# Attention's side jobs in a four-layer Flamingo kernel: stages written by an estimate of each engine's progress instead of by counts of ticks

## The chip, the cores and the metric

The kernel runs on one core of one Trainium2 chip. The metric is device time in microseconds (us), of which lower is better. The kernel is one program with one launch; it reads all its inputs from the chip's memory and writes its output there.

## The reference, cut to what matters

Sixteen batches of 128 tokens with 256 features go through four layers. Each layer adds a gated attention to a second sequence (`ctx_1024`) and then a gated feed-forward part. All arithmetic is in float32.

```python
x = x + tanh(g_xattn[0]) * L0_xattn(ctx, layernorm(x), ctx)   # 16 heads, width 16
x = x + tanh(g_ffn[0])   * L0_ffn(layernorm(x))               # 8 experts, top 2, hidden 1024, gelu
x = x + tanh(g_xattn[1]) * L1_xattn(layernorm(x), ctx, ctx)   # softmax over the queries
x = x + tanh(g_ffn[1])   * L1_ffn(layernorm(x))               # a dense product and 8 gated LoRA experts
x = x + tanh(g_xattn[2]) * L2_xattn(ctx, ctx, layernorm(x), mask)
x = x + tanh(g_ffn[2])   * L2_ffn(layernorm(x))               # 8 experts, top 2, swiglu, and a shared expert
x = x + tanh(g_xattn[3]) * L3_xattn(ctx, layernorm(x))        # 8 heads of 64; keys from ctx and from x
x = x + tanh(g_ffn[3])   * L3_ffn(layernorm(x))               # 8 experts, top 2, silu

# one of the expert parts: a router, the two best experts of a token, their outputs weighted
gate = softmax(x @ w_gate.T); scores, idx = top_k(gate, 2)
cw = (one_hot(idx, 8) * scores[..., None]).sum(1)
h = gelu(einsum('td,edh->teh', x, W1) + b1)
out = einsum('ted,te->td', einsum('teh,ehd->ted', h, W2) + b2, cw)
```

## The kernel before, in words

**Batches, blocks and steps.** The sixteen batches lie in four blocks of four (`NBLK`, `BPB`). One function, `attend` (L1302), writes the attention of a layer, and it is called three times: for layer 0, for layers 1 and 2 one after the other ("the middle"), and for layer 3. It goes through steps. Step n writes the scores of batch n (`scores`: products L1211 into `ps_s`, exponentials L1221 and L1226 into `e`), the values of batch n-1 (`values`: products L1266 of `e` with `v`, then with `ones` for the row sums, a reciprocal L1277, and `oT`, L1274 or L1279), and the output of batch n-2 (`output`: product L1287 into `ps_y`, then additions into the residual `x`, L362 and L366, and the layer norm's statistics in `ready`). On POOL the row sums are kept in `sum_range` (L1080). Layer 3 has a class of its own for these, `Fast3`.

**The order is written out by hand.** Inside `attend` TensorE (PE), ScalarE (ACT) and VectorE (DVE) are under `tc.manual_schedule`: they execute their instructions in the order in which Python writes them. GpSimd (POOL) and SyncE (SP) also take theirs in program order, outside the three queues. An instruction that waits holds up all that is behind it on its engine.

**Side jobs.** Between the parts of a step stand the stages of other work, each job a Python generator whose `yield` ends a stage:

- queries and keys of the next block (L1155 to L1181, products L929 and L932, `v` in L941 and L947); in layer 3 `turned`, `projected` and their context (L1820 to L1890);
- the layer norm of a finished block, `ln_block` (L316: `xn` on ACT L306, transposes `ps_ln` L329, copy L333);
- the front of the experts for a finished block, `Moe.front` (L436): the layer norm, router (L413), softmax, two maxima (`hot`, `both` L464), ranks (`ps_rank`, L469), offsets and the list of places `xi` (L505 to L521), eight indirect scatters of the tokens into `xg` in memory (L524, POOL), and after some blocks a plan;
- the LoRA part of layer 1 (`Lora.run`, L1453) and the shared expert of layer 2 (`shared2`, L1521);
- slots of expert work (`slots`, L703). A slot is 128 gathered tokens of one expert: it loads `xr` from `xg` (L752) and the first weights (L1373, 1 MB in layer 0) by SP's queue, transposes `xr` (L785), makes the hidden layer (L1420, L1597 or L1645), then the second product (`ps_e`, L822), and scatters the result (L834). There are 39 slots per expert layer. Layer 0 runs 9 of them early, inside its attention, once the plan of blocks 0 and 1 is there; layer 3 runs 9 and then 8 early; the others come after the attention.

**What sets their order before the change.** `attend` calls `tick()` some six times in each step: between the two halves of the scores and after them, between values and row sums and after them, and in `output`. Each job holds a counter; a tick takes one off, and at zero the next stage is written and its `yield` sets the counter anew (`yield 4`: four ticks on). The argument `most` caps the counter: (5, 1) in layer 0, (99, 1) in the middle, (2, 1) in layer 3, the second number once the last scores are written. `Firm` numbers escape the cap, and `quick` cuts a front's numbers to 3. All jobs run at each tick, as many as there are. A stage is thus written a fixed number of ticks after the one before, whether or not its inputs are there yet by then; and the products of a job stand between the halves of a batch's scores, or between its values and row sums, where their tiles have another shape: scores use 32-row tiles (`32*128`), values 32-column tiles (`128*32`), all else is `128*128`.

Of the kernel before, what the change touches and what calls it, by code (L numbers as in the profile page):

```python
# [19 lines left out]
P = 128  # L20
# [70 lines left out]
def kernel(ctx: ExitStack, tc: tile.TileContext, a: dict, out: bass.AP):  # L91
# [112 lines left out]
    class Firm(int):  # L204
        pass

    def quick(job):

        for n in job:
            yield min(n, 3)  # L210
# [41 lines left out]
    seen = {}  # L252

# [44 lines left out]

    def normalized(srcs, mv, rstd):
# [3 lines left out]
        yield 1  # L303
        xns = stat.tile([P, len(srcs), ROW], F32, tag="xn", name="xn", bufs=3)
        for i, src in enumerate(srcs):
            nc.scalar.activation(  # L306
                xns[:, i, 0:D], src, AF.Identity, bias=nmr[:, i:i + 1], scale=rstd[:, i:i + 1]
            )
            if i == 1:
                yield 1  # L310
# [5 lines left out]
    def ln_block(blk, see=None, own_set=False):  # L316
# [6 lines left out]
        yield Firm(3) if own_set else 4  # L323
        xt = xtpool.tile([P, KC, TB], F32, tag="xnT", name="xnT")
        for pair in range(BPB // 2):
# [8 lines left out]
            yield 1 if pair == 0 else 3  # L334
# [87 lines left out]
    class Moe:  # L422
# [4 lines left out]
        def __init__(self, layer, wg, turn, see=None):  # L427
            self.layer, self.wg, self.turn, self.see = layer, wg, turn, see
            self.carry = region
            self.done = None  # L430
            self.scatters, self.returns, self.weighted = [], [], []
# [4 lines left out]
        def front(self, blk, plan=None):  # L436
# [3 lines left out]
            xns, xnT = yield from ln_block(blk, self.see, own_set)  # L440
# [24 lines left out]
            yield Firm(2) if own_set else 6  # L465
# [37 lines left out]
            yield 3  # L503
            off = small("off")
# [17 lines left out]
            for i in range(BPB):  # L522
                for j in range(2):
# [3 lines left out]
                    ).ins, self.scatters, "scatter")  # L527
            if plan is not None:
                yield 1
                yield from plan()  # L530
            return xnT
# [158 lines left out]
        def slots(self, n, plans, lanes, get, fetch1, fetch2, hidden, nf, far, depth):  # L690
# [149 lines left out]
            while not planned(far):  # L840
                yield 1
# [7 lines left out]
            yield 1  # L849
# [3 lines left out]
            for s in range(n):  # L853
                while not planned(s + far + 1):
                    yield 1
# [11 lines left out]
                yield 1  # L867
# [230 lines left out]
    class Fast16:  # L1098
# [44 lines left out]
        def keys(self, blk):  # L1143
# [3 lines left out]
            for c in range(KC):  # L1147
# [8 lines left out]
                yield 1  # L1156

        def queries(self, blk, before):
# [8 lines left out]
            for c in range(KC):  # L1167
# [13 lines left out]
                yield 2  # L1181

        def scores(self, b, tick):
# [24 lines left out]
            for c in range(KC):  # L1208
# [6 lines left out]
                if c == 0:  # L1215
                    tick()
# [29 lines left out]
            tick()  # L1246
# [7 lines left out]
        def values(self, b, tick):  # L1254
            pool, v = self.pool, self.vs[b % 3]
            es = self.es.pop(b)
            oT = pool.tile([P, KC, S], F32, tag="oT", name="oT")
# [3 lines left out]
            for i in range(1 if self.layer == 1 else 2):  # L1261
# [9 lines left out]
                if i == 0:  # L1271
                    tick()
# [10 lines left out]
        def output(self, b, tick):  # L1283
            oT = self.os.pop(b)
            py = ps_x.tile([P, D], F32, tag="x", name="ps_y")
# [16 lines left out]
    def attend(parts, most=(99, 1), filler=None, open_end=False):  # L1302
# [7 lines left out]
        jobs = []  # L1310
        late = False
        filling = []

        def tick():
            for job in list(jobs) + filling:
                job[1] -= 1
                if job[1] <= 0:
                    try:
                        n = next(job[0])
                        job[1] = n if isinstance(n, Firm) else min(n, most[late])  # L1320
                    except StopIteration:
                        (jobs if job in jobs else filling).remove(job)

        def ahead(att, before, blk):
            made = att.prepare(blk, before(blk) if before is not None else None)
            made = [[job, 0] for job in made]
# [5 lines left out]
                  for blk in range(NBLK)]  # L1332
        with tc.manual_schedule(engines=IN_ORDER):
            ln_exp()
            prepared = ahead(*blocks[0][:2], 0)
            for n in range(len(steps) + 2):
                if n == len(steps) - 1 and open_end:
                    next(filler)
                if n == len(steps):
                    late = True  # L1340
                    if filler is not None:
                        filling.append([filler, 0])
                if n < len(steps):
                    if n % BPB == 0:

                        while any(job in jobs for job in prepared):
                            tick()
                        if n // BPB + 1 < len(blocks):
                            att, before, _, blk = blocks[n // BPB + 1]
                            prepared = ahead(att, before, blk)  # L1350
                    att, b = steps[n]
                    att.scores(b, tick)
                if 1 <= n <= len(steps):
                    att, b = steps[n - 1]
                    att.values(b, tick)
                if n >= 2:
                    att, b = steps[n - 2]
                    att.output(b, tick)
                    if b % BPB == BPB - 1:
                        _, _, behind, blk = blocks[(n - 2) // BPB]  # L1360
                        jobs.append([behind(blk), 0])
            while jobs or (filling and not open_end):
                tick()
# [37 lines left out]
    def slots0(moe, n, plans, lanes, get):  # L1401
# [10 lines left out]
        def hidden(get, w, xT, when):  # L1412
            hT = get("hT", [P, nf, S])
            for half in range(2):
# [13 lines left out]
                yield 1  # L1428
# [5 lines left out]
    class Lora:  # L1434
# [10 lines left out]
        def run(self, blk):  # L1445
# [20 lines left out]
            yield 8  # L1466
# [8 lines left out]
            yield 5  # L1475
            for i, b in enumerate(block(blk)):
# [10 lines left out]
                yield 1  # L1487
# [949 lines left out]
```

## Time and profile before

| what | value |
|---|---|
| median of three runs | 1697.64 us (1696.58 to 1700.13) |
| the profiled execution, its own time | 1650.85 us |
| its span, first to last instruction | 1648.8 us |
| mean clock granted to TensorE | 0.973 of full |
| PE busy | 1536.8 us, 93% of the span |
| DVE busy | 874.5 us, 53% |
| ACT busy | 635.8 us, 39% |
| POOL busy | 319.0 us, 19% |

The profile and the trace record one execution. It is 46.8 us shorter than the median of the timed runs, so differences found in the trace are made against 1650.85 us and then carried over to the median. A row of the profile's groups gives the line and engine of an instruction, the tile that it writes and those that it reads, how often it runs, its busy time, the mean time of one, and the idle time just before it with the engine and line that ended it. The rows of stages that the prediction shows give, for each stretch of time, the busy time of the five engines, the granted clock and the share of the DMA engines.

### The profile page before, as it was taken

The numbers are of one execution on the slowest core, as the hardware profiler recorded it, in microseconds if no ns is written. First come the engines' busy times: TensorE is split into PE (matmuls) and PEld (weight loads), VectorE is DVE, ScalarE is ACT, GpSimd is POOL, SyncE is SP. The second block draws the span as 40 slices with busy tenths as digits, with TensorE's granted clock in tenths as the row PEclk, the third lists the DMA queues.
The fourth block names the chain that finished last, engine by engine and source line by source line (L and its number), as shares of the span: only waits on it lengthen the run. The fifth ranks groups of instructions, "written<-read, shape, count | busy, mean of one in ns | idle before, by whom it ended". The sixth has DMA issues, their size and how long they took to land.

```text
span 1648.8 us, 34904 instructions
## 1 busy us (share of the span) xinstructions
PE 1536.8 (93%) x12803; PEld 1194.4 (72%) x12803; DVE 874.5 (53%) x2860; ACT 635.8 (39%) x1517; POOL 319.0 (19%) x402
## 2 busy tenths in 40 slices
PE   6988999999988999999999999999989999998992
PEld 4677889999455666655459999999946655667892
DVE  3686322422367756764445555556734526466655
ACT  4545433345455455553224333334443333223110
POOL 4132411111600000221100110111150002023431
PEclk8998999999999999999999999999989999998997
DMA  9606584443600000110055413401260000033866
GB/s 337 235 31 199 187 268 155 146 146 93 119 1 1 1 14 14 40 40 26 26 208 163 137 58 106 151 27 34 97 122 1 15 1 27 1 98 123 272 188 207
DMA packets 108200, 169.68 MB, mean 103 GB/s; under 512 B 17129, under 2 KB 78382, under 8 KB 108016
## 3 DMA queue, kind: packets, MB, share of 16 engines
q1 hardware_dynamic: 84176, 112.38, 21.6%
q0 software_dynamic: 20304, 49.66, 9.6%
q10 hardware_dynamic: 3536, 5.25, 0.9%
q8 instruction: 108, 1.77, 0.5%
q14 instruction: 76, 0.62, 0.1%
HBM read 268.81 MB, written 48.18 MB: 192 GB/s over the span
## 4 chain that ended last, share of the span: by engine, by line


## 5 line engine op out<-in xcount | busy, mean ns | idle before, releaser
L1597 PEld LDWEIGHTS ps_w<-xT,w 128*128 128x128 f32 x2304 | 264.0, 192 | 2.5
L1597 PE MATMUL ps_w<-xT,w 128*128 128x128 f32 x2304 | 264.9, 275 | 0.0
L834 POOL DMA_INDIRECT yd<-y,to x117 | 119.2, 1019 | 562.8 <-DVE c L797 285.7
L822 PE MATMUL ps_e<-w,hT 128*128 128x256 f32 x848 | 197.5, 380 | 1.8 <-DVE hT L1502 1.3
L822 PEld LDWEIGHTS ps_e<-w,hT 128*128 128x128 f32 x848 | 154.5, 190 | 21.0 <-DVE hT L1502 2.3
L1605 ACT ACTIVATE u<-ps_w,b 128x128 f32<-128x128 f32 x312 | 89.2, 368 | 172.7 <-PE ps_w L1597 165.4
L1608 DVE SCALAR_TENSOR_TENSOR m<-ps_w,b,u 128x128 f32<-128x128 f32 x312 | 87.7, 344 | 111.0 <-PE ps_w L1597 94.0
L1420 PE MATMUL ps_h<-xT,w 128*128 128x128 f32 x1120 | 134.8, 279 | 7.9 <-DMA w<-in_l_w_dram 6.5
L1420 PEld LDWEIGHTS ps_h<-xT,w 128*128 128x128 f32 x1120 | 132.9, 196 | 11.0 <-issue 4.3
L1425 ACT ACTIVATE hT<-ps_h,b 128x128 f32<-128x128 f32 x312 | 88.9, 373 | 114.3 <-issue 83.5
L524 POOL DMA_INDIRECT xg<-xn,xi x96 | 94.2, 981 | 152.9 <-ACT u L1538 55.0
L1532 PE MATMUL ps_w<-xnT,sw 128*128 128x512 f32 x256 | 111.9, 593 | 0.0
L830 DVE SCALAR_TENSOR_TENSOR y<-ps_e,c,bias 128x256 f32<-128x256 f32 x78 | 37.6, 482 | 126.4 <-PE ps_e L822 125.2
L1080 POOL TENSOR_TENSOR sum_range<-sum_range,rs 128x256 f32<-128x256 f32 x48 | 35.1, 732 | 342.2 <-DVE rs L1277 155.3
L1532 PEld LDWEIGHTS ps_w<-xnT,sw 128*128 128x128 f32 x256 | 47.9, 190 | 57.3 <-issue 50.9
L306 ACT ACTIVATE xn<-x,nmr,rstd 128x256 f32<-128x256 f32 x128 | 67.8, 598 | 30.9 <-DVE nmr L302 30.9
L787 DVE COPY xT<-ps_xr 128x256 f32<-128x256 f32 x117 | 48.5, 417 | 57.7 <-PE ps_xr L785 57.6
L1277 DVE RECIPROCAL rs<-ps_o 128x256 f32<-128x256 f32 x32 | 56.2, 1756 | 42.8 <-PE ps_o L1266 42.8
L1211 PE MATMUL ps_s<-qM,kT 32*128 32x256 f32 x768 | 68.9, 418 | 5.2 <-ACT e L1226 5.2
L1226 ACT ACTIVATE e<-ps_s 128x512 f32<-128x512 f32 x128 | 65.7, 602 | 11.4 <-PE ps_s L1211 11.4
L814 ACT ACTIVATE bias<-b,c 128x256 f32<-128x256 f32 x78 | 40.4, 517 | 73.0 <-DMA b<-in_l_b_dram 28.9
L1854 PE MATMUL ps_qk<-kvx,w_att 128*128 128x512 f32 x128 | 62.7, 624 | 0.6 <-DVE kvx L1841 0.6
(275 smaller groups left out, 2547.6 us busy)
## 6 DMA issues: line engine op xcount, KB each, us to landing
w<-in_l_w_dram SPq DMA_DIRECT2D x156, 1024.0 KB
w<-in_l_w_dram SPq DMA_DIRECT2D x39, 512.0 KB
kT<-in_l_wgu_dram SPq DMA_DIRECT2D x39, 512.0 KB
xg<-zeros POOLq DMA_DIRECT2D x15, 1170.0 KB, 24.0
xr<-xg SPq DMA_DIRECT2D x78, 130.0 KB
b<-in_l_b_dram SPq DMA_DIRECT2D x78, 128.0 KB
kT<-in_l_w_dram SPq DMA_DIRECT2D x39, 256.0 KB
x<-yd POOLq DMA_DIRECT2D x48, 128.0 KB, 4.8
```

Source lines behind the costliest of these rows:

```text
L306: nc.scalar.activation(xns[:, i, 0:D], src, AF.Identity, bias=nmr[:, i:i + 1], scale=rstd[:, i:i + 1])
L524: self.unordered(nc.gpsimd.indirect_dma_start(out=xg[:, :], in_=xns[:, i, :], in_offset=None, out_offset=bass.IndirectOffsetOnAxis(ap=xi[: ...
L822: nc.tensor.matmul(po, lhsT=hT[:, f, :], rhs=lane(s)["w2"][:, f, :], start=(f == 0), stop=(f == nf - 1),)
L834: self.unordered(nc.gpsimd.indirect_dma_start(out=yd[:, :], in_=y, in_offset=None, out_offset=bass.IndirectOffsetOnAxis(ap=to[:, 0:1], axi ...
L1211: nc.tensor.matmul(pss[j][:, 2 * c:2 * c + 2, :], lhsT=self.kT[blk][part, c, tok], rhs=self.qM[blk][part, c, :, tok], start=True, stop=True,)
L1226: nc.scalar.activation(e, pss[j], AF.Exp)
L1420: nc.tensor.matmul(ps[:, i, :], lhsT=w["w1"][:, k, f * P:(f + 1) * P], rhs=xT[:, k, :], start=(k == 0), stop=(k == KC - 1),)
L1425: nc.scalar.activation(hT[:, f, :], ps[:, i, :], AF.Gelu, bias=w["b1"][:, f:f + 1])
L1532: nc.tensor.matmul(ps, lhsT=wt[:, k, f * P:(f + 1) * P], rhs=xnT[:, k, :], start=(k == 0), stop=(k == KC - 1),)
L1597: nc.tensor.matmul(ps[:, f, :], lhsT=wt[:, k, s, f * P:(f + 1) * P], rhs=xT[:, k, :], start=(k == 0), stop=(k == KC - 1),)
L1605: nc.scalar.activation(u[:, f, :], pair[0][:, f, :], AF.Identity, bias=w["b1"][:, i:i + 1])
L1608: nc.vector.scalar_tensor_tensor(m1[:, f, :], pair[1][:, f, :], w["b3"][:, i:i + 1], u[:, f, :], ALU.add, ALU.mult,)
```

## The change

Counters go; an estimate of time comes. While `attend` runs, a callback hands each written instruction to a new class `Clock`, which holds a time for each of the four compute engines and for each tile (when it will be written, until when it is read), and adds a formula's duration per instruction. A stage of a job is now marked by its `yield`: `yield Pe(0)` or `yield Pe(1)` says that the stage that follows writes products to PE, a plain number that it doesn't. `Pe(1)` waits in the estimate for what the last stage made, `Pe(0)` doesn't. The rules:

- a stage without products is written at any tick (`poll`) as soon as the estimated PE time has passed the estimated end of its inputs;
- a stage with products is written only at whole ticks (`whole`): one ahead of a step's scores, one after its output; and only until a budget of `share` us of PE time per step is used up: 2.5 in layer 0, 5.0 in the middle, 8.0 in layer 3;
- the ticks inside the scores, between scores and values, and between values and row sums become `tick(False)`, which only polls;
- ahead of the values (`until(v, *es)`) and of the output (`until(oT)`) ready PE stages are written as long as the estimate says that those tiles aren't there yet (`idle`), the filler too;
- `urgent` writes, ahead of the values, ready PE stages of a finished block's job, where `hurry` is set (it is, in all three calls);
- at most two jobs of finished blocks are open at once (`waiting`), the third begins when the first has ended; a front takes up the running offsets only when the front before it has finished (`self.passed`), `xn`'s three buffers are handed on only when released (`held`), and layer 2's block is held until layer 1's LoRA part of that block has been written (`through`);
- early slots of layer 0 wait by `while not started: yield Pe(1)`.

What is computed, the tiles, the loads and the number of instructions of each kind stay as they were; their order changes. The core of the diff:

```diff
-    def attend(parts, most=(99, 1), filler=None, open_end=False):
...
-        def tick():
-            for job in list(jobs) + filling:
-                job[1] -= 1
-                if job[1] <= 0:
-                    try:
-                        n = next(job[0])
-                        job[1] = n if isinstance(n, Firm) else min(n, most[late])
+    class Clock:
...
+        def note(self, ins):
+            outs, srcs = self.aps(ins.outs), self.aps(ins.ins)
...
+            if "DMA" in type(ins).__name__ or ins.engine not in self.at:
+                end = max(start, self.at[PE]) + 3.0
+                self.moved.append(end)
+            else:
+                start = max(start, self.at[ins.engine])
+                end = start + self.cost(ins, outs[0], srcs)
+                self.at[ins.engine] = end
+                end += 0.2 if ins.engine == PE else 0.1
+                self.ends.append(end)
...
+    def attend(parts, filler=None, open_end=False, hurry=True, share=2.5):
...
+        def run_stage(job):
+            clock.ends, clock.moved = [], []
+            try:
+                n = next(job[0])
...
+            job[2] = isinstance(n, Pe)
+            ends = clock.ends or clock.moved
+            if not ends:
+                job[1] = now() + (0.5 if n else 0.0)
+            else:
+                job[1] = max(ends) if n else now()
...
+        def poll():
+            while True:
+                for job in list(jobs):
+                    if not job[2] and job[1] <= now():
+                        run_stage(job)
+                        break
+                else:
+                    return
+
+        def whole():
+            poll()
+            for job in jobs:
+                if job[2] and job[1] <= now() + 0.1:
+                    run_stage(job)
+                    return True
+            return False
...
+            def __call__(self, full=True):
+                if not full:
+                    poll()
+                    return
+                end = now() + self.left
+                while now() < end and whole():
+                    pass
+                self.left = end - now()
+                poll()
...
+            def until(self, *tiles):
+                t = clock.when(*tiles)
+                while now() < t:
+                    idle(t)
...
             for n in range(len(steps) + 2):
+                tick.left = share
...
+                    tick()
                     att, b = steps[n]
                     att.scores(b, tick)
                 if 1 <= n <= len(steps):
+                    tick.urgent()
                     att, b = steps[n - 1]
                     att.values(b, tick)
...
-                        jobs.append([behind(blk), 0])
+                        job = begin(behind(blk), False, hurry)
+                        waiting.append(job)
+                        if len(waiting) <= 2:
+                            jobs.append(job)
+                    tick()
```

and in the jobs, for example:

```diff
-        yield Firm(3) if own_set else 4
+        yield Pe(1)
...
-            yield Firm(2) if own_set else 6
+            yield Pe(1)
...
+            while self.passed < blk:
+                yield 1
             off = small("off")
...
-                    tick()
+                    tick(False)
...
+            tick.until(v, *es)
...
-                    attend([(att, clear, behind)], (5, 1), early())
+                    attend([(att, clear, behind)], early())
...
-                    attend(parts, filler=most_shared())
+                    attend(parts, most_shared(), share=5.0)
...
-                        [(att, lambda blk: moe2.fetch(pool, blk), behind)], (2, 1), job, True
+                        [(att, lambda blk: moe2.fetch(pool, blk), behind)], job, True, share=8.0
```

## The prediction

> **What bounds the kernel now.** I read the page's engine totals and slices first, then the table of stages, then PE's waits inside single stages, then timelines around the worst of them. The chain that ended last is empty on this page, so the bound has to come from the other views.
>
> ```profile
> PE 1536.8 (93%) x12803; PEld 1194.4 (72%) x12803; DVE 874.5 (53%) x2860; ACT 635.8 (39%) x1517; POOL 319.0 (19%) x402
> ...
> PEclk8998999999999999999999999999989999998997
> ```
>
> PE bounds it: 93% busy, the next engine 53%. The change adds no product and takes none away, so a gain can only come from PE's idle time (1648.8 - 1536.8 = 112 us), from spells at a lower granted clock, and from PE time that is lost inside busy groups. Where does that idle time lie? In the stages' rows below, columns are the length, then busy time of PE, PE's weight loads, DVE, ACT and POOL, the clock, the DMA share and GB/s.
>
> ```profile
> 40.00:124.00 84.00, 77.41 (x1151) 56.35 (x1149) 62.89 (x186) 41.71 (x88) 20.03 (x24) 0.98 0.36 137
> 124.00:157.00 33.00, 26.74 (x255) 21.44 (x255) 21.61 (x83) 17.05 (x36) 8.75 (x10) 0.84 0.69 226
> 157.00:240.00 83.00, 77.56 (x520) 72.03 (x519) 26.72 (x134) 33.75 (x98) 25.68 (x26) 0.98 0.70 231
> ...
> 445.00:730.00 285.00, 266.00 (x2804) 176.42 (x2803) 193.34 (x531) 151.75 (x294) 35.80 (x51) 0.99 0.07 18
> ...
> 1478.00:1560.00 82.00, 68.44 (x523) 61.94 (x512) 55.60 (x277) 16.58 (x31) 31.31 (x33) 0.90 0.54 172
> ```
>
> The first row is layer 0's attention, the second its tail where the early slots start, 445 to 730 the middle (layers 1 and 2), the last the tail of layer 3's attention. PE's idle time (length less busy) is 6.6, 6.3, 5.4, 19.0 and 13.6 us. The slots between (240 to 417, 730 to 1200) are full, 0 and 6 us, and lie outside `attend`. The start (0 to 40, 13 us) and the end (1560 to 1648, 29 us) wait for the first inputs and the last results, which the change doesn't reach. So some 60 us of `attend` are open to it, its layer-3 body (1200 to 1478: 8.8 us) included. In the middle, the waits of PE are these (total, times, longest):
>
> ```profile
> PE ps_ln L329 <- ACT xn L306: 3.2, 3, 1.7
> PE ps_o L1266 <- DVE oT L1279: 2.6, 3, 1.8
> PE ps_ln L329 <- ACT oT L1274: 1.9, 1, 1.9
> PE ps_zT L1470 <- ACT oT L1274: 1.9, 1, 1.9
> PE ps_v L947 <- DVE qM L1172: 1.8, 2, 1.4
> ```
>
> Many short waits, no single cause: a product stood in PE's queue before its input was there, while DVE (193 of 285 us) and ACT (152) had slack. This is what counting ticks gives, and what an estimate can avoid. The timeline of PE in layer 0 shows a second loss:
>
> ```profile
> 41.99 1.15 PE L1211 MATMUL ps_s<-qM,kT 32*128 32x256 f32 x16
> ...
> 46.37 1.02 PE L929 MATMUL ps_k<-ctxT,w_att 128*128 128x512 f32 x2
> 47.32 0.71 PE L1211 MATMUL ps_s<-qM,kT 32*128 32x256 f32 x8
> 47.96 1.13 PE L929 MATMUL ps_k<-ctxT,w_att 128*128 128x512 f32 x2
> ```
>
> Scores in one piece take 1.08 us from start to the next start (41.99 to 43.07 in that timeline), in two pieces with a job between 0.64 each (47.32 to 47.96): 0.20 us more for two more changes of tile shape, **0.1 us per change**.
>
> **What the Trainium skill says.** "TensorEngine Tiling (Array Packing)", Key Properties: switching the tiling mode drains TensorE. It gives no price; the 0.1 us above agrees. "TensorE: Matmul & The Clock Gate", Part 1, What's actually happening: after an idle window of about 3.4 us the rate halves, and it takes about as long of busy time to return. The trace agrees in kind: after 2.63 us of idle at 127.6 the values take 1.94 us at 132.03 against 1.08 at 137.50, and the stage's clock is 0.84. So an idle spell costs itself and some 1.7 us more (half of 3.4). "DMA: Bandwidth & Descriptors", Anatomy of one DMA: about 2.0 us are fixed, mostly the receipt. Here the last scatter ends at 131.46 and the load behind it is issued at 133.33, 1.9 us.
>
> **The change part by part,** against the profiled execution (1650.85 us; span 1648.8).
>
> *Fewer shape changes.* In the two written orders of PE I counted changes of tile shape: 220 before and 159 after in layers 0 to 2, and some 45 fewer in layer 3's attention. (61 + 45) x 0.1 = 10.6 us, on PE itself, so all on the path; about 2 in layer 0, 4 in the middle, 4.5 in layer 3.
>
> *The middle.* Idle 19.0 plus 0.01 x 266 = 2.7 us of clock: 21.7. Stages of LoRA, layer norm and queries now stand together and only when the estimate has their inputs, and `until` puts ready work ahead of values whose `e` is late. I take two thirds, 14 us, because the estimate's formulas aren't the chip's and one product early still holds the queue. With the 4 for shapes: **-18** (range -8 to -26). What becomes late: the layer norm of the next block's first queries just ahead of its first scores, where `attend` must finish the prepared jobs whatever there is to do. Estimate 1 to 2 us each, twice; in the range and in the shading below.
>
> *Layer 0 and its handover.* This is the part that can lose. The first 9 slots need the plan of blocks 0 and 1, and so front 1. Before, front 1's ranks are written ahead of batch 13's scores; after, behind batch 14's values, since PE stages keep to 2.5 us per step. Its scatters are 8 instructions on POOL, with 1.275 us from one to the next:
>
> ```profile
> 121.54 0.99 POOL L524 DMA_INDIRECT xg<-xn,xi  x1 [5.08 <-DVE xi L521]
> ...
> 130.49 0.97 POOL L524 DMA_INDIRECT xg<-xn,xi  x1 [0.30 <-DVE rs L1277]
> ```
>
> ```profile
> 133.33 0.37 SPq L752 DMA_DIRECT2D xr<-xg  x1
> 134.65 0.38 SPq L1373 DMA_DIRECT2D w<-in_l_w_dram  x1
> ```
>
> ```profile
> 141.25 2.05 PE L1420 MATMUL ps_h<-xT,w 128*128 128x128 f32 x16 [0.52 <-DVE xT L787]
> ...
> 151.83 4.55 PE L1420 MATMUL ps_h<-xT,w 128*128 128x128 f32 x25 [1.93 <-DMA w<-in_l_w_dram]
> ```
>
> From `xi` to the first slot's product this chain has 0.8 (POOL takes it up) + 9.9 (eight scatters) + 1.9 (receipt) + 1.3 (to the weights' issue) + 6.6 (to L1420) = 20.5 us, and the second slot follows 10.6 us later, for weights. Before, PE still had two and a half batches to write under that chain. In the order after, with t the end of batch 14's output, `xi` comes at t + 3 to 4 and only the last output and the ranks (0.97 + 0.36 us) are left: PE idles for about 20 us, then some 6 for the second slot, with 1.7 of half clock after each: about 29.5 of loss. Before, PE's loss from 0 to 240 is, group by group (start to next start, less the shortest of the same group), 47.4 us: 13.1 in the first 40 us, 13.3 up to 120, 21 after that. After: 13.1 stays; 2 for 40 to t, since no side job waits then; 29.5; and about 1 beyond, because front 3's ranks move from behind the sixth early slot to behind the second, so that its plan is ready some 40 us sooner and the waits at 222 and 228 (0.7 and 2.4 us, with L1420 at half clock, 5.1 against 3.6) go. 45.6 against 47.4: **-2** (range -6 to +6). Each us by which t comes later than 121 (105.9 of PE work, 13.1 and 2 of loss) adds one; it turns into a loss of this stage at t = 123.
>
> *Layer 3.* Body: 4.5 for shapes and part of 8.8 us of waits, most for `xn` (5.1 us): **-6** (range -2 to -10). Tail: 13.6 idle and 0.10 x 68 = 6.8 of clock. The fronts of blocks 2 and 3 come earlier by whole stages; the longest waits are for `xn` (4.3), a slot's `xT` (3.6) and its rows (2.4), and the first two are side jobs put before their inputs: **-10** (range -4 to -16). Here the same chain (scatters to slot) stays covered, with some 30 us of products of attention behind front 1's ranks against the 20.5.
>
> Sum: -18 - 2 - 6 - 10 = -36; less 3 for new waits at the block boundaries and at jobs that come too early, -33: 1618 us for the profiled kind of execution, a ratio of 0.980. Carried to the median: 1697.64 x 0.980 = **1664 us**.
>
> **Rivals.** (a) *New waits eat most of it*: the estimate is off on DVE or ACT and stages stand before inputs as often as before, so that only the shapes and the plan's move remain, -8 to -16: 1680 to 1690. For it: the formula for a DMA is a flat 3 us, where weights here take 7 to 9. Against: most jobs in `attend` hang on ACT and DVE rather than on loads. (b) *Nearly all is recovered*, shapes and all 60 us of idle but for the handover: -48 to -58, about 1640 to 1648. Against: the handover alone keeps 29. (c) *Slower, by the handover*: t slips because 2.5 us per step also pushes front 1's earlier stages, to t = 133 (all of before's losses up to there plus nothing won), PE idles 20 + 6 us with little to cover, and layer 0 loses 10 while the middle merely exchanges one set of waits for another: 1651 + 10, 1708 in the median. It decides when the other stages gain less than t - 123. Against: the middle's waits have no single cause that could come back whole. (d) *The order doesn't do what it says*: excluded for the shapes by the count; if nothing else came of it, it is (a).
>
> **How the numbers follow.** 0.2%, 3.4 us, is about what a measurement of this kernel can tell from no change. Likeliest case (1650 to 1680, centre 1664) 0.62; (a), up to 1694, 0.16; (b) 0.08; within 0.2%, 0.04; slower, (c), 0.10. Faster: 0.62 + 0.16 + 0.08 = 0.86. The range leaves out (c) and the no-change case: 1640 to 1694.
>
> **What would show it.** PE busy about 1535 less some 10; the middle 12 to 20 us shorter with its `ps_ln` and `ps_zT` waits mostly gone; scores as x16 groups throughout; a hole of about 20 us in PE ahead of the first L1420, a second of about 6, clock under 0.8 there, and then no wait at the main slots' first weights; the tail of layer 3 without 3 to 4 us waits. Wrong would be: a middle as long as before, with `ps_o` waiting for `e` each step (nothing now stands between scores and values), or a hole ahead of L1420 of over 30 us.

## The result, and the profile after

| kernel | median, us | runs |
|---|---|---|
| before | 1697.11 | 4 (1696.31 to 1700.13) |
| after | 1669.09 | 4 (1667.73 to 1669.38) |

The ratio is 0.983 (95% interval 0.981 to 0.985): 28 us faster. All times of this study lie at one of two levels, the same one throughout a group of runs: the kernel before takes about 1650 us at "level A" and about 1698 at "level B". The recorded expectations speak of two chips, but the record has chip 10 and later 11 at level A, and chip 10 and later 13 at level B: what sets the level isn't shown. The profile of before shown ahead of the prediction is from an execution at level A, the times above and the profile of after are of level B. These two profiles are therefore not compared in time (1650.85 and 1668.93 us look like a loss), only in form; sizes come from kernels traced at one level.

The page of after, engine totals:

```profile
PE 1531.7 (92%) x12803; PEld 1202.6 (72%) x12803; DVE 876.6 (53%) x2860; ACT 630.7 (38%) x1510; POOL 318.8 (19%) x402
```

The number of products is as before. PE's busy time is 5 us less, across the levels; at level A the same order (l0_share8, below) has 1512.1 us, 24 less than the order of before there (1536.1 in all_counted). ACT has seven instructions fewer, though the change was to leave their number alone: it loads its function tables 21 times instead of 28. By stages (same stretches as before, columns as there: length, busy PE, PE's loads, DVE, ACT, POOL, clock, DMA share, GB/s), profile of after:

```profile
40.00:124.00 84.00, 77.53 (x1163) 57.79 (x1161) 59.54 (x157) 45.03 (x92) 19.03 (x24) 0.96 0.35 134
124.00:157.00 33.00, 13.02 (x182) 10.21 (x174) 23.31 (x111) 7.45 (x16) 9.83 (x11) 0.67 0.42 140
157.00:240.00 83.00, 71.22 (x463) 66.57 (x464) 21.81 (x111) 32.20 (x91) 22.52 (x23) 0.92 0.63 211
```

The second row is the handover to the early slots in layer 0: PE is busy 13 of 33 us at a clock of 0.67, where before it was 26.7 at 0.84. It is the hole that the prediction placed there. The waits of PE in the middle, profile of after (total, times, longest):

```profile
PE ps_ln L334 <- DVE x L375: 2.5, 1, 2.5
PE ps_o L1281 <- issue: 2.0, 4, 1.0
PE ps_ln L334 <- ACT xn L311: 1.5, 2, 1.2
PE ps_ln L334 <- DVE oT L1294: 1.1, 2, 0.6
```

The waits for `xn` and those of `ps_zT` have shrunk, and a new one of 2.5 us for `x` stands at a block's boundary. All groups of scores stand unsplit (x16) in the order after.

### The profile page after: what moved, and what is told of

It reads as the page before. It is cut to its first block, busy times and chain, and to the rows that moved or that the text cites. A ratio compares the mean times of both kernels' runs of the same rounds, so it can differ in the third digit from the quotient of the medians.

```text
span 1667.1 us, 34912 instructions
## 1 busy us (share of the span) xinstructions
PE 1531.7 (92%) x12803; PEld 1202.6 (72%) x12803; DVE 876.6 (53%) x2860; ACT 630.7 (38%) x1510; POOL 318.8 (19%) x402
## 4 chain that ended last, share of the span: by engine, by line
## 5 line engine op out<-in xcount | busy, mean ns | idle before, releaser
L311 ACT ACTIVATE xn<-x,nmr,rstd 128x256 f32<-128x256 f32 x128 | 68.3, 602 | 23.0 <-DVE nmr L304 13.8
L1225 PE MATMUL ps_s<-qM,kT 32*128 32x256 f32 x768 | 60.7, 417 | 2.8 <-ACT e L1240 2.8
L240 DVE BATCH_NORM_STATS2 bnst<-x 128x6 f32<-128x256 f32 x128 | 53.8, 420 | 8.6 <-DMA x<-in_x_dram 5.6
```

Source lines behind the costliest of these rows:

```text
L311: nc.scalar.activation(xns[:, i, 0:D], src, AF.Identity, bias=nmr[:, i:i + 1], scale=rstd[:, i:i + 1])
L1225: nc.tensor.matmul(pss[j][:, 2 * c:2 * c + 2, :], lhsT=self.kT[blk][part, c, tok], rhs=self.qM[blk][part, c, :, tok], start=True, stop=True,)
```

## The experiments

For separate layers I wrote a file that holds both rules. Each `yield` carries both numbers (`Pe(1, 4)`: by the estimate 1, by counting 4), and beside `attend` stands `attend_counted`, the function of before; each of the three calls takes one of them. The lengths in this table are read from the traces, between first or last products: layer 0 up to the last L1420 of before's numbering (the hidden layers of its slots), the middle up to the first L1597, the slots of layer 2 up to the first L1830, layer 3's attention up to the last L2030, and the rest up to the last product.

| kernel | level | layer 0 | middle | slots of 2 | attention 3 | rest |
|---|---|---|---|---|---|---|
| all_counted | A | 411.2 | 454.7 | 332.9 | 294.6 | 125.1 |
| all_counted_2 | A | 413.6 | 454.7 | 332.9 | 294.7 | 124.7 |
| only_l0 | A | 425.0 | 458.6 | 332.9 | 294.8 | 124.5 |
| only_mid | A | 412.2 | 432.0 | 333.6 | 289.9 | 123.7 |
| only_l3 | A | 413.4 | 454.8 | 332.9 | 266.7 | 128.1 |
| l0_share8 | A | 421.7 | 438.7 | 333.6 | 266.9 | 128.3 |
| handover_whole | A | 411.7 | 438.5 | 333.6 | 266.9 | 127.1 |
| after | B | 434.2 | 445.5 | 333.6 | 283.2 | 141.4 |
| after_again | B | 434.3 | 439.2 | 333.6 | 282.0 | 142.1 |
| l0_counted | B | 429.8 | 443.7 | 333.6 | 282.0 | 142.3 |
| front_whole | B | 429.4 | 445.1 | 333.6 | 283.4 | 141.7 |
| counted_direct | B | 428.2 | 470.5 | 333.2 | 294.4 | 131.9 |
| fronts_whole | B | 432.6 | 438.8 | 333.6 | 289.5 | 126.1 |

### One layer at a time

```diff
-                    attend([(att, clear, behind)], early())
+                    attend_counted([(att, clear, behind)], (5, 1), early())
...
-                    attend(parts, most_shared(), share=5.0)
+                    attend_counted(parts, filler=most_shared())
...
-                        [(att, lambda blk: moe2.fetch(pool, blk), behind)], job, True, share=8.0
+                        [(att, lambda blk: moe2.fetch(pool, blk), behind)], (2, 1), job, True
```

With all three lines the order is that of before ("all_counted"); each of the other kernels leaves one of the three calls as the change has it.

> The new file with all three attention calls put back to the counting of ticks: every engine's order is that of the kernel before. It asks where the 46 us lie by which the timed runs of before (1697) are longer than the one execution of it that was traced (1651). Theory A: the traced execution was a lucky one and an ordinary one loses the 46 us in a few places, which the trace will show; 1695 to 1700 us. Theory B: the trace is true and the timed runs are longer by something outside the program's instructions: the span is again 1649 with 1697 timed.

> The estimate rules in layer 0's attention only, counting in the middle and in layer 3. By my prediction (layer 0 about even) 1694 to 1698 us; by the two traces, in which layer 0's early slots end 20.7 us later than before, 1715 to 1720 us; if the 46 us of ordinary runs of before were lost in layer 0 and the change recovers them, 1670 us.

> The estimate rules in layers 1 and 2 only. By my prediction 18 to 20 us less than before, 1677 to 1680 us; by the two traces, in which this stage with its filler gains 9 us, 1688 us; if the 46 us lie here, 1650 us.

> The estimate rules in layer 3 only. By my prediction 16 us less than before, 1681 us; by the two traces, in which this stage is 6 us longer, 1703 us; if the 46 us lie here, 1655 us. If the three parts add up, the differences of these three runs sum to the whole difference, -28 us.

Measured at level A, before at 1650.3: all_counted 1651.4 (ratio 1.0004, 0.998 to 1.002); only_l0 1666.6 (1.009, 1.007 to 1.012); only_mid 1629.2 (0.989, 0.982 to 0.995); only_l3 1627.0 (0.986, 0.981 to 0.991). So +16, -21 and -23 us, in sum -28, the difference that the change makes at level B. (The middle's -21 is the least certain: its four runs lie between 1621 and 1638, its interval between -8 and -30.) Both theories of the first expectation miss: before isn't lucky in one execution, all its 20 runs here take about 1650, and the span agrees with the timed runs.

Where does the middle's gain lie? PE's waits there, all_counted:

```profile
PE ps_ln L344 <- ACT xn L321: 5.7, 4, 2.5
PE ps_s L1806 <- DVE hTs L1753: 2.8, 2, 1.4
PE ps_o L1291 <- DVE oT L1304: 2.7, 3, 1.8
```

and only_mid, the same stage:

```profile
PE ps_s L1806 <- DVE hTs L1753: 2.8, 2, 1.4
PE ps_ln L344 <- DVE x L385: 2.5, 1, 2.5
PE ps_ln L344 <- ACT xn L321: 1.5, 2, 1.2
```

The waits for `xn` and `oT` shrink; the shared expert's two waits for `hTs` stay. Reckoned as in the prediction (time from one group's start to the next less the shortest of the same form, here over all four traces), PE loses about 52 us before and 33 after in the middle, and 49 and 26 in layer 3; the sums move by 1 to 5 us with the way groups are cut. About half of this is idle time: PE's idle time falls from 26.4 to 15.1 us in the middle and from 23.9 to 14.0 in layer 3 (all_counted, only_mid, only_l3). The rest lies inside PE's busy time: 38 and 24 changes of tile shape fewer, in layer 3 also 14 us less at a granted clock of one half (27.3 to 13.7; it differs between executions, 6.8 in only_mid with layer 3 counted). Three of the seven table loads that fall away are in the middle and one in layer 3, at 1.28 us of ACT each; no run sets them apart from the rest.

Layer 0's loss shows in PE's timeline of only_l0:

```profile
125.03 2.08 PE L1313 MATMUL ps_y<-w_att,oT 128*128 128x256 f32 x4 [0.55 <-DVE oT L1304]
133.38 0.64 PE L489 MATMUL ps_rank<-both,tri 128*128 128x32 f32 x2 [6.28 <-DVE both L484]
...
143.75 0.66 PE L809 MATMUL ps_xr<-ident,xr 128*128 128x128 f32 x2 [9.30 <-DMA xr<-xg]
148.05 5.80 PE L1670 MATMUL ps_h<-xT,w 128*128 128x128 f32 x32 [3.63 <-DMA w<-in_l_w_dram]
156.06 0.98 PE L809 MATMUL ps_xr<-ident,xr 128*128 128x128 f32 x4 [2.21 <-DMA xr<-xg]
160.61 6.32 PE L1670 MATMUL ps_h<-xT,w 128*128 128x128 f32 x32 [3.57 <-DMA w<-in_l_w_dram]
...
233.24 3.81 PE L1670 MATMUL ps_h<-xT,w 128*128 128x128 f32 x32 [0.73 <-issue]
236.89 0.38 PE L809 MATMUL ps_xr<-ident,xr 128*128 128x128 f32 x2
239.85 5.44 PE L1670 MATMUL ps_h<-xT,w 128*128 128x128 f32 x32 [2.58 <-DMA w<-in_l_w_dram]
```

The attention's last output is written at 125 us; in all_counted the first slot starts at 140.8 and batch 15's output follows at 148.6. With the estimate the attention thus ends some 23 us sooner, but the work that would follow isn't there: 6.3 us for front 2's maxima, 9.3 for the rows, 3.6 for the weights, then the same for the second slot, with hidden layers of 5.8 and 6.3 us at granted clocks of 0.64 and 0.58 (3.8 at full). The rows from 233 on are the first slots after the nine early ones: the second still waits for its weights.

### The parts together, and layer 0 put back

> The changed kernel as it is, beside before on one chip. On the chip of the last runs before took 1650 us and not 1697; the differences of the three layers there (+16, -21, -23) sum to -28 us. If the parts add up and the chip matters only as an offset, 0.983 of before again: 1622 us on a chip where before takes 1650.

> Layer 0's attention by counting, the other two calls by the estimate. My theory (layer 0's handover costs 16 us, all of it in the wait for the first two slots): 44 us below before, 1606 where before is 1650, and faster than the changed kernel by 16. Rival (the layers' gains overlap, for instance by the clock or by what is left for the filler): within 5 us of the changed kernel.

l0_counted puts back the first of the three lines above. At level B, before at 1698.1: after_again 1663.6 (0.981, 0.978 to 0.985), l0_counted 1665.7 (0.983, 0.979 to 0.988). The first came as expected. The second is a miss: putting back layer 0, worth 16 us at level A, is worth nothing that can be told apart here, and its trace has layer 0 only 4.5 us shorter (429.8 against 434.3). At level B counting loses time in layer 0 that it doesn't lose at level A (411 to 414 us).

### What makes the handover late

In front_whole front 1 of layer 0 (`whole = self.layer == 0 and blk == 1`) writes its work after the router in one stage; handover_whole does so with the plan behind it as well; fronts_whole with every front and plan of layers 0 and 3 (`whole = self.layer != 2`). l0_share8 changes the budget alone.

```diff
             soft = softmax8(lg)
             next(soft)
-            yield 1
+            if not whole:
+                yield 1
             next(soft)
...
-            yield 3
+            if not whole:
+                yield 3
             while self.passed < blk:
...
-            yield 1
+            if not (self.layer == 0 and early):
+                yield 1
             part = t([P, NE, NE], "part")
```

```diff
-                    attend([(att, clear, behind)], early())
+                    attend([(att, clear, behind)], early(), share=8.0)
```

> The changed kernel, but front 1 of layer 0 writes its DVE work after the router in one stage instead of five (no yields between logits, softmax, maxima; none between ranks and offsets). Theory A (the handover is late because each of these stages waits for a whole step, 4.5 us): front 1's scatters come some 14 us sooner, the hole ahead of the first slot shrinks by as much, 12 to 15 us less than the changed kernel. Theory B (what the prediction said: the budget of 2.5 us of PE per step holds the front back): no gain beyond 3 us.

> The changed kernel, with front 1 of layer 0 and its plan each written in one go (no yields between the DVE stages of either). With the front alone in one go the scatters came 14 us sooner but the first slot's rows only 3.5, since the plan's five stages, one per step, came last. Theory A (stages written one per step are what makes the handover late): the first slot's product 12 to 15 us sooner than in the changed kernel, layer 0 shorter by 10 to 15, so 1650 us where the changed kernel takes 1664. Theory B (something behind it takes the wait's place at once: the weights' load, or the end of the scatters): 5 us or less.

> The changed kernel with a budget of 8.0 instead of 2.5 us of PE per step in layer 0. The prediction held the budget responsible for front 1's late ranks: then the ranks come a step or two sooner and layer 0 gains 5 to 9 us. If it is the one stage per step of the front's and the plan's DVE work: within 3 us of the changed kernel.

> The order of before once more, for its trace. Where before takes 1698 us (it took 1650 on one chip and 1698 on another), theory A: the trace shows 48 us more than the one with 1650, spread over the attentions as short stops of PE inside groups of one kind that are put down to issue (27 us in the changed kernel there, 6 us on the other chip). Rival: the 48 us lie in one place, or outside PE's stops, in the stages with the expert slots alone.

front_whole, at level B: 1660.3 (0.978, 0.974 to 0.982), 3 us below after_again and not to be told from it. Its scatters begin at 123.44 instead of 137.83, as theory A had it, but the first slot's rows are asked for only 3.3 us sooner (147.86 instead of 151.11). Its timelines of DVE and of SP's queue tell what came in between:

```profile
146.89 0.18 DVE L688 CAST plan_i<-plan 128x36 int32<-128x36 f32 x1
```

```profile
147.86 0.36 SPq L772 DMA_DIRECT2D xr<-xg  x1
```

The load needs the plan, and the plan's five stages were still written one per step. The other three ran at level A, before at 1650.7. handover_whole: **1606.2 us** (0.973, 0.970 to 0.976). l0_share8: 1620.5 (0.981, 0.978 to 0.984), the same ratio as the changed kernel. In its trace the instructions of PE, ACT, DVE and POOL come in the changed kernel's order, so the budget of 2.5 us never held a stage back, and l0_share8 is the changed kernel measured at level A: 30 us faster than before. all_counted_2, run once: 1652.4; as the level was A again, it couldn't say where level B's 48 us lie, which stays untraced for the kernel before. PE's timeline in handover_whole:

```profile
124.86 1.13 PE L1315 MATMUL ps_y<-w_att,oT 128*128 128x256 f32 x4
130.11 0.43 PE L811 MATMUL ps_xr<-ident,xr 128*128 128x128 f32 x2 [2.23 <-DMA xr<-xg]
134.14 3.48 PE L1596 MATMUL ps_h<-xT,w 128*128 128x128 f32 x16 [3.60 <-DMA w<-in_l_w_dram]
137.45 1.89 PE L1315 MATMUL ps_y<-w_att,oT 128*128 128x256 f32 x8
```

The first slot starts at 134.1 instead of 147.7 (l0_share8), the last two outputs lie behind it as cover, and layer 0 is 10.0 us shorter, the kernel 14. Theory A holds. The budget is not the cause of the late ranks: in l0_share8 front 1's ranks stand where they stood with a budget of 2.5. From l0_share8 and from only_l0, in that order:

```profile
117.16 0.41 PE L479 MATMUL ps_rank<-both,tri 128*128 128x32 f32 x2
```

```profile
117.14 0.41 PE L489 MATMUL ps_rank<-both,tri 128*128 128x32 f32 x2
```

> Every front and every plan of layers 0 and 3 in one go, not only front 1 of layer 0. With front 1 and its plan alone the ratio to before was 0.973 (0.970 to 0.976), where the changed kernel has 0.981 to 0.983. Theory A (stages one per step cost only where a handover hangs on them with PE idle behind it): layer 3's early slots start after the last attention step whatever the fronts do, so 0.970 to 0.976 again. Theory B (the same lateness costs in layer 3's tail, where PE waits 7 us for a slot's rows): 5 to 8 us less, 0.968 or below. A loss would be the lumps of DVE work holding up the reciprocals of layer 3, above 0.977.

At level B, before at 1698.7: 1657.1 (0.977, 0.974 to 0.981). The ratio that theory B named (0.968 or below) doesn't come. Between theory A and a loss by lumps of DVE work the interval doesn't decide, and the level is the other one. The trace divides it otherwise than theory A: layer 3, its attention and the rest together, takes 415.6 us, against 424.1 to 425.1 in the four traces of level B with its fronts as in the change. That is the size of theory B's gain, but not shown to be its cause: eight of the 32 scatters have moved from the rest into the attention, and waits of 8.5 us for a slot's `xT` and 6.6 for its `code` stand in the tail. In layer 0 the first slot starts 15 us sooner than in after_again (142.4 against 157.5) and yet layer 0 ends only 1.7 us sooner. The last section tells what took its place.

### Direct order without the estimate

```diff
-        def count():
+        def count(full=True):
             for job in list(jobs) + filling:
                 job[1] -= 1
-                if job[1] <= 0:
+                if job[1] <= 0 and (full or not job[2]):
```

(`job[2]`: the next stage has products; `through` and `passed` hold here as in the change.)

> Counting in all three calls, but a counted stage with products may be written only after a batch's values and after its output, not inside scores or between values and row sums: the half of the change that lets values follow scores directly, without the estimate (changes of tile shape in PE's order 276 before, 185 here, 191 in the changed kernel). If shapes are worth 0.1 us each: 8 to 9 us below before at most. If it is the direct order that brings the gain of the middle and of layer 3: 35 to 45 us. If stages then come too late and PE waits for them: above before.

At level B 1687.8 (0.994, 0.992 to 0.995): 10.3 us below before, against 34.5 for the changed kernel in the same comparison. That is what 91 changes of tile shape fewer would give at 0.1 us (9.1), though stages that come later in this kernel are in the sum as well. The direct order is about a third of the gain; the rest came only with the estimate. Which of the estimate's rules brings it (`until`, `urgent`, two jobs at most) was not taken apart. Between counted_direct and after_again, both at level B, the middle is 31 us shorter, 470.5 to 439.2; before has no trace at that level to set beside them.

## Why the prediction was right, and where it was not

1664 us was forecast and 1669 measured, in the likeliest case (1650 to 1680); the ratio is 0.983 where the text had 0.980. The terms can be set beside traces at level A only. There, between all_counted_2 and l0_share8, layer 0 takes 8.1 us more, the middle 16.0 less and layer 3 24.2 less, where the text had -2, -18 and -16, and 3 for new waits: that the sum came out is partly luck, since layer 0's error is made up for in layer 3. At level B, for which the time was forecast, before has no trace; with layer 0 counted (l0_counted) the other two calls gain 32 us (34 in the text), and layer 0 adds nothing that can be told apart. The terms one by one:

- **Shapes**, -10.6: counted in the traces as for counted_direct, the change takes away 85 changes of shape and not 106 (24 in layer 3, where the text had some 45), 8.5 us at the same price. The price agrees with counted_direct (91 fewer, -10.3), at level B and with the reservation above.
- **The middle**, -18: measured -22.7 in the trace of only_mid (454.7 to 432.0) and -21 timed, but -16 in l0_share8 and handover_whole (438.7 and 438.5), where it has the same order. The clock lies between them: PE stood at half clock for 6.8 us of the middle in only_mid and for 20.5 in the other two (13.7 in all_counted), and half of that difference is 6.9 us. Without these spells it would be about -19 in all three, an estimate from these figures. The mechanism is as written: short waits for `xn` and `oT` go, one of 2.5 us at a block's boundary is new, which was the rival within the step.
- **Layer 0**, -2 (range -6 to +6): wrong at level A, +13.8 in the trace of only_l0 and +16 timed, +8.1 in l0_share8 with the same order, against all_counted_2. The hole itself was predicted well (20 + 6 us, first L1420 some 24 us behind batch 14's output; measured 6.3 + 9.3 + 3.6 = 19.2 and 2.2 + 3.6 = 5.8 us, 25.4 from 122.7 to 148.05). What failed are the terms around it. The loss between 40 us and batch 14's output was put at 2 us since no side job would wait there; it is 8.5. The loss beyond the handover was put at 1 us, since front 3's earlier ranks should make its plan some 40 us earlier and the main slots' waits go; it is 10. The plan comes only 17 us earlier (192.4 against 209.7 in all_counted), and both waits are still there (0.73 and 2.58 us against 0.74 and 2.51): the plan was not what they hung on. The load of weights at 221.84, behind which SP's later loads stand, waits 3.5 us for an earlier slot's second product, with the plan there for 29 us. The seventh early slot waits for weights as well (2.9). Each of the two terms is 6 to 9 us off. The handover costs 32.4 and not 29.5; the 1.7 us of half clock behind each stop, an estimate, came out as 2.0 and 2.5. At the start 9.9 are lost instead of 13.1. Together 61.7 us against 48.3 before, where the sum had 45.6 against 47.4.
- **The reason given for the late ranks**, PE's budget of 2.5 us per step, was wrong: l0_share8 has the same order with 8.0. It is the DVE stages without products, as front_whole and handover_whole show. A stage can be written only once the estimate has the one before done, DVE's queue of attention work ahead of it included, so that each of the front's stages takes a step of 4.5 us. From router to `xi` it takes 26.9 us in only_l0 (100.8 to 127.6), 12.9 in all_counted (108.9 to 121.7).
- **Layer 3**, body -6 and tail -10: together -16, measured -24.9 (419.7 to 394.8, some 7 of it less time at half clock), divided otherwise: -27.9 and +3.0. The first slot product stood 12.4 us ahead of the attention's last output and now stands 6.2 behind it, so slot work moved from the body into the tail. That the tail's long waits would go was wrong: the wait for `xn` goes, one of 5.2 us for a slot's `xT` takes the place of one of 3.6. In only_l3:

```profile
1464.17 4.07 PE L2287 MATMUL ps_y<-w_att,oT 128*128 128x256 f32 x16
1468.08 0.30 PE L489 MATMUL ps_rank<-both,tri 128*128 128x32 f32 x2
...
1474.01 2.07 PE L1897 MATMUL ps_g<-xT,kT 128*128 128x128 f32 x8 [5.16 <-DVE xT L811]
```

The rivals: (a) and (b) didn't come about. Of (c) the uncovered stop came, but neither its cause (a t put off by the budget) nor its outcome: layer 0 cost 16 us at level A, more than the 10 given there, but the other two calls gained 44 together. Its turning point depended on t, and t was on time (122.7 us); the loss came with t on time, so the point was set at the wrong quantity.

## What to carry to other kernels

An in-order engine gains from an order in which work is written when its inputs are due, but an order that packs an engine tighter brings forward the moment at which it runs out of work; look up what the next stage hangs on, here a chain of scatters, plan and weights, and move that chain first. A chain of small stages, each written only when the last is done, costs a scheduling step per stage whatever its stages cost: write those on the way to a handover in one go. And compare traces only within one level of the same kernel's time: here the profile of the faster kernel was 18 us longer than that of the slower one.

## What the runs showed of the hardware

Before takes some 48 us longer at level B, the changed order 41 to 48 in the traces (1662.0 and 1668.9 against 1620.8). This isn't spread evenly: the slots of layer 2, the only stage of the table without scatters into `xg`, take 333.6 us at both levels, to the tenth (they have 38 single scatters of results), while layer 0, the middle and layer 3's two parts take 9 to 13, 1 to 7, 15 to 16 and 13 to 14 us more (after and after_again against l0_share8, for layer 0 against only_l0 as well; the order is the same). At level B PE stops again and again inside groups of one form while POOL issues eight scatters. After, PE's timeline during its scatters (92.56 to 102.6):

```profile
94.72 0.39 PE L1281 MATMUL ps_o<-e,ones 128*32 128x128 f32 x6
...
96.80 0.42 PE L1281 MATMUL ps_o<-e,ones 128*32 128x128 f32 x4 [0.32 <-issue]
97.51 0.27 PE L1281 MATMUL ps_o<-e,ones 128*32 128x128 f32 x1 [0.29 <-issue]
98.24 0.41 PE L1281 MATMUL ps_o<-e,ones 128*32 128x128 f32 x3 [0.46 <-issue]
```

Those 32 row sums take 8.4 us up to the next product (94.72 to 103.10). During only_l0's scatters of the same front (92.14 to 102.1, level A) they take one:

```profile
94.30 1.06 PE L1291 MATMUL ps_o<-e,ones 128*32 128x128 f32 x32
95.28 1.13 PE L1313 MATMUL ps_y<-w_att,oT 128*128 128x256 f32 x4
```

Other engines stop with it. In fronts_whole two fronts' scatters follow one another (169 to 190 us), and from 178 to 193 PE gets one product every 1.4 to 2.1 us, and DVE one or two small operations in about that time. DVE's timeline there:

```profile
178.99 0.29 DVE L626 TENSOR_TENSOR past<-have,fills 128x128 f32<-128x128 f32 x1 [1.18 <-DVE have L622]
179.31 0.29 DVE L631 TENSOR_REDUCE cnt<-past 128x8 f32<-128x128 f32 x1
180.40 0.17 DVE L637 TENSOR_TENSOR left<-cnt,done 128x8 f32<-128x8 f32 x1 [0.81 <-DVE cnt L631]
180.49 0.16 DVE L638 TENSOR_SCALAR skip<-cnt 128x8 f32<-128x8 f32 x1
181.83 0.17 DVE L639 TENSOR_TENSOR skip<-skip,done 128x7 f32<-128x7 f32 x1 [1.18 <-DVE skip L638]
```

This took 14 us of what the earlier handover had won in that kernel. In all, PE's stops inside groups come to 26 to 34 us in the six traces of level B and to 6 to 12 in the eight of level A. Between after or after_again and l0_share8 they are 15 to 16 us more (27.5 and 27.1 against 11.7), so they are a third of what level B costs there; the rest isn't traced to a place.

What holds the engines isn't shown. The shortest of these intervals, 1.4 us, lie near the scatters' own 1.28 from one to the next. But during the first of the two fronts' scatters, from 169 to 178, PE ran a hidden layer's 32 products in 3.82 us, as it does without scatters. And in the list of DMA queues the two that carry instructions moved nothing during the stops (92.5 to 105 in after, 175 to 193 in fronts_whole), which doesn't decide whether instructions came late. Why one level shows it and the other doesn't stays open, and so does why counting has no advantage left in layer 0 at level B.
